# Weights of an attention layer multiplied by Strassen's scheme on pairs of row tiles, with additions moved to GpSimd and side jobs spread anew, in a two-layer graph kernel

## Chip, cores and metric

The kernel runs on one core of a Trainium2 chip. The metric is the device time of one execution in microseconds (us); the time before is the median of three runs, 2179.1 us (2177.47 to 2179.86).

## What is computed

x has 3327 rows of 512 numbers, adj is 3327 x 3327, everything in float32. With h = relu(layernorm(x)), layer 0 is graph attention and layer 1 a normalised graph convolution:

```
h = relu(layernorm(x))
q, k, v = h Wq' + bq, h Wk' + bk, h Wv' + bv
x = x + softmax(q k' / sqrt(512) + 2 adj) v
h = relu(layernorm(x))
A2 = adj + I;  ds = diagonal(A2) ** -0.5
x = x + relu((ds A2 ds) (A2 h W'))
```

## The kernel before

**Tiles.** Rows are padded to 26 tiles of 128. They are kept as two halves of 13 tiles (six pairs and one left over) and as two strips s = 0 and 1, of 14 and 12 tiles; matmuls have 448 columns for strip 0 and 384 for strip 1. `ROW` gives the order in which row tiles are finished.

**Opening (lines 273 to 379).** Wq and Wk are merged into one matrix M. For each of the 26 row tiles, `h_transposed` loads x, computes the norm (`norm`, L191: statistics on VectorE, the power -0.5 on GpSimd at L200, and on demand the bias -mean * rstd on VectorE, L204), applies relu with scale and bias on ScalarE (ACT, L323), stores h for later and transposes it on TensorE. `project_q` multiplies by M. In this part the instructions are put in order by a scheduler at build time.

**Scores (lines 384 to 577).** Products of h and q, exp, and stores of the probabilities and of sums of blocks that Strassen's scheme needs, into DRAM.

**Three big products (from line 581).** g = 0 is probabilities times h, g = 1 is A2 times h of layer 1, g = 2 is A2 times the rows of layer 1's product. Each is done by one level of Strassen's scheme over halves (seven products p5, p1, p6, p7, p2, p3, p4, `ORDER`), with a second level inside. A **step** is one of these products for one strip and one pair of row tiles: `Step`, with seven matmuls (L813) or, for the thirteenth tile, four (L805). Steps are numbered by `number_of(g, r, s, t)`: 98 for each g, 14 for each of the seven products, 7 for each strip. `Right` makes a step's right side out of stored rows, `Gather` takes the finished strip out of PSUM (`first`, `rest`) and `settle` combines strips into `cts`.

Order is written out by hand: `run(k)` issues step k's loads (for step k+3), its matmuls, and between the matmuls pieces of VectorE's work from the list `waiting` (sums of step k+2, then what `at(k, ...)` has put there); `in_order` pins each engine's instructions, including DMA issues on SP and ACT, to that order. `post` and `deliver` put ACT's stores off to the next step.

**Layer 0's weights** (what the change replaces). The result of g = 0 stands transposed in `cts`. For each row tile, at steps 79 to 108, `attend` multiplies four slices of it by Wv (`times_weights`, four matmuls of 512 columns, L905), and VectorE scales the sum by rs and adds x (L917), adds bv (L918) and takes the norm's statistics; x comes by `attend_load` on ACT's queue two steps earlier, and `attended` applies relu on ACT one step later and stores h of layer 1 (`rowd[1]`).

**Layer 1's weights.** `Temp` (L939) does the same kind of product for pairs of row tiles by seven products of half size with the blocks of W and their sums (`W`, `four_differences`), at places between matmuls given by `AFTER`: eight additions of 128x128 on VectorE (`sums`, L956), 14 matmuls of 256 columns (L966), four evictions on ACT (L970) and three on VectorE (L972).

**Side jobs.** `Job` (L881) adds a block of adj to a stored sum and stores the result, for later products of g = 1 and 2: two loads on SP, one VectorE addition (L896), one store on ACT. There are 52, evenly spread over steps 7 to 163, in four places (two jobs deep).

Of the kernel before, what the change touches and what calls it, by code (L numbers as in the profile page):

```python
# [15 lines left out]
P = 128  # L16
# [20 lines left out]
PAIRS = 6  # L37
# [10 lines left out]
def graph_layers_kernel(  # L48
# [117 lines left out]
    totd = dram.tile([1, NP], F32, name="totd")  # L166
    x1d = [dram.tile([P, D], F32, name=f"x1d{i}") for i in range(NT)]
# [23 lines left out]
    def norm(src):  # L191

        st = small.tile([P, 6], F32, name="st")
        nc.vector.bn_stats(st, src)
        mv = small.tile([P, 2], F32, name="mv")
        nc.vector.bn_aggr(mv, st)
        ve = small.tile([P, 1], F32, name="ve")
        nc.vector.tensor_scalar(ve, mv[:, 1:2], EPS, None, op0=ALU.add)  # L198
        rstd = small.tile([P, 1], F32, name="rstd")
        nc.gpsimd.tensor_tensor(rstd, ve, mhalf, op=ALU.pow)  # L200

        def bias():
            nb = small.tile([P, 1], F32, name="nb")
            nc.vector.scalar_tensor_tensor(nb, mv[:, 0:1], -1.0, rstd, op0=ALU.mult, op1=ALU.mult)  # L204
            return nb

        return rstd, bias
# [85 lines left out]
    nc.sync.dma_start(bq_sb, bq)  # L293
    M = blocks(range(4, 8), "M")
# [20 lines left out]

    def h_transposed(k):

        a, n = PACKS[k]
        for _, i in (o for o in order if o[0] == k):
# [3 lines left out]
            nc.scalar.activation(ht, xt, AF.Relu, bias=bias(), scale=rstd)  # L323
            nc.sync.dma_start(rowd[0][ROW[i]], ht)
            pt = tp_bank("tp").rearrange("p (c e) -> p c e", c=DC)
# [50 lines left out]
    for k, then in itertools.zip_longest(TURN, TURN[1:]):  # L376
        if then is not None:
            h_transposed(then)
        project_q(k)
# [240 lines left out]
    def weights(src):  # L620

        w = [half(k, [P, 2, D], "w") for k in (12, 13)]
        for c in range(DC):
            nc.sync.dma_start(w[c // 2][:, c % 2], src[c * P : (c + 1) * P])
        return [w[c // 2][:, c % 2] for c in range(DC)]

# [3 lines left out]
    bvs = []  # L630

    def prepare():
        wv_w1.append(weights(wvT))
        bvs.append(half(11, [P, D], "bv_sb"))
        nc.sync.dma_start(bvs[0], bass.AP(tensor=bv.tensor, offset=bv.offset, ap=[[0, P], [1, D]]))
        LD = adjT.shape[1]
        with nc.allow_non_contiguous_dma(reason="the diagonal, once"):
            nc.sync.dma_start(dg, bass.AP(tensor=adjT.tensor, offset=adjT.offset, ap=[[LD + 1, P], [P * (LD + 1), NT]]))

    def prepared():  # L640
        nc.vector.reciprocal(rs, tot)
        nc.vector.tensor_scalar(dg, dg, 1.0, None, op0=ALU.add)
        nc.gpsimd.tensor_tensor(sd, dg, mh, op=ALU.pow)
        nc.scalar.mul(nsd, sd, -1.0)

    wv_w1 = []
# [3 lines left out]
    def other_weights():  # L650

        b11, b21, b22, t1, t2, t3 = blocks((11, 12, 13), "w1")
        b12, t4 = (mid(k, [P, 2, E], "w1") for k in (10, 11))
        W.extend((b11, b12, b21, b22, t1, t2, t3, t4))
        for z in range(2):
            for y in range(2):
                block = w1T[z * E : (z + 1) * E, y * E : (y + 1) * E]
                nc.sync.dma_start(W[2 * z + y], block.rearrange("(c p) e -> p c e", p=P))
        differences.append(four_differences(W))
# [7 lines left out]
    nsd = const.tile([P, NT], F32, name="nsd")  # L667

# [37 lines left out]
    job_ring = ring(*spare[2:], (half, 14))  # L706
    x_slots = [lambda k=k: view(2, 1).rearrange("p a w -> p (a w)")[:, k * D : (k + 1) * D] for k in range(3)]
    x_slots = itertools.cycle([*x_slots, lambda: mid(10, [P, D], "xt")])
    h_ring = ring((mid, 11))
# [171 lines left out]
    class Job:  # L881


        def __init__(self, k, s, j):
            self.k, self.s, self.j = k, s, j

        def load(self):
            s, j, w = self.s, self.j, H[self.s]
            self.a, self.b = (job_ring([P, H[0]], "job")[:, :w] for _ in range(2))
# [11 lines left out]
    def times_weights(i, w):  # L901
        s, y, k = where(i)
        ps = bank(ROLE["p8"], "p8")
        for d in range(DC):
            nc.tensor.matmul(ps, cts[s][y][d][:, k * P : (k + 1) * P], w[d], start=d == 0, stop=d == DC - 1)  # L905
        return ps

    xts = {}

    def attend_load(i):  # L910
        xts[i] = next(x_slots)()
        nc.scalar.dma_start(xts[i], x[i * P : (i + 1) * P])

    def attend(i):

        xt, ps = xts[i], times_weights(i, wv_w1[0])
        nc.vector.scalar_tensor_tensor(xt, ps, rs[:, i : i + 1], xt, op0=ALU.mult, op1=ALU.add)  # L917
        nc.vector.tensor_add(xt, xt, bvs[0])  # L918
        post(x1d[i], xt)
        normed[i] = norm(xt)  # L920

    def attended(i):
        h1 = h_ring([P, D], "h1")
        nc.scalar.activation(h1, xts[i], AF.Relu, bias=normed[i][1](), scale=normed[i][0])
        nc.scalar.dma_start(rowd[1][i], h1)

    normed = {}

# [10 lines left out]
    class Temp:  # L939
# [10 lines left out]
        def sums(self):  # L950

            a11, a12, a21, a22 = self.blocks()
            self.o = half(14, [P, 4, 2, P], "rows")
            for k, x, y in ((1, a21, a22), (2, None, a11), (3, None, a12), (0, a11, a21)):
                for c in range(2):
                    yield nc.vector.tensor_add(self.o[:, k, c], self.o[:, {2: 1, 3: 2}[k], c] if x is None else x[c], y[c])  # L956

        def product(self, j):
            name, h, new, n, sign = PARTS[j]
            if j == 0:  # L960
                self.ps = bank(ROLE["p8"], "pw").rearrange("p (k e) -> p k e", k=2)
                self.to = [next(ts_slots)() for _ in self.its]
            left, ps = {"m1": 0, "p2": 1, "p4": 3}.get(name), self.ps[:, h]
            for c in range(2):
                a = self.o[:, {"p7": 0, "p5": 1, "p6": 2, "p3": 3}[name], c] if left is None else self.blocks()[left][c]
                nc.tensor.matmul(ps, a, W[B[name]][:, c], start=new and c == 0, stop=c == 1, skip_group_check=True)  # L966
            i = self.its[n // 2]
            to, by = self.to[n // 2][:, n % 2 * E : (n % 2 + 1) * E], (sd if sign > 0 else nsd)[:, i : i + 1]
# [4 lines left out]
            if j == len(PARTS) - 1:  # L973
                for i, ts in zip(self.its, self.to):
                    post(rowd[2][i], ts)
# [40 lines left out]
    every = (*range(PAIRS), None)  # L1016
    rights = {(g, r, t): Right(g, r, t) for g in range(3) for r in ORDER for t in every}
# [23 lines left out]
    k0, k1 = number_of(0, 0, 1, 0), number_of(1, 5, 0, 0) - 4  # L1041
    for n, job in enumerate(jobs):
        k = k0 + n * (k1 - k0) // len(jobs)
# [3 lines left out]
    def rows(g, k, i, *z):  # L1047

        if g == 0:
            at(k - 2, attend_load, i)  # L1050
            at(k, attend, i)
            at(k + 1, attended, i)
        else:
            at(k - 2, finish_load, i, *z)
            at(k, finish, i, *z)
# [3 lines left out]
    k = number_of(0, 5, 1, 2)  # L1059
    for i in ROW:  # L1060
        if steps[k].t is None:
            k += 1
        rows(0, k, i)
        k += 1
    inserted, sums_of = {}, {}
    k = number_of(1, 5, 1, 2)
    for n in range(0, NT, 2):
        if steps[k].t is None:
            k += 1
        w = Temp(*ROW[n : n + 2])  # L1070
        sums_of[k] = w.sums
        for j, (later, m) in enumerate(AFTER):
            inserted.setdefault((k + later, m), []).append((w, j))
        k += 2
# [11 lines left out]
    for t, i in enumerate(range(20, NT)):  # L1086
        rows(2, number_of(2, 4, 0, t + 2), i, (1,))
# [4 lines left out]
    k = number_of(1, 4, 0, 0)  # L1092
    at(k, other_weights)
    for n in range(4):
        at(k + 3 + n, difference)
    at(k + 8, turn_sign)
# [27 lines left out]
    def run(k):  # L1124
# [19 lines left out]
        for j, _ in enumerate(itertools.chain((None,), step.multiply(banks_of))):  # L1144
# [11 lines left out]
            elif weighs and j > 0:  # L1156
# [29 lines left out]
        while len(waiting) > added:  # L1186
            do(waiting.pop(0))

# [384 lines left out]
```

## Time and profile before

| what | value |
|---|---|
| median of three runs | 2179.1 us |
| the profiled execution's own time | 2178.22 us |
| its span (first to last instruction) | 2176.4 us |
| TensorE's granted clock | 0.997 |
| ACT busy | 238.4 us (11%) |
| L905, 512 columns, cts by Wv | part of 104 matmuls, two passes each |
| DMA moved | 583.68 MB, mean 268 GB/s |
| GpSimd pow at L200 | 52, mean 0.83 us |

Times are microseconds on one profiled execution. PE is TensorE's matmul, PEld its weight load, DVE VectorE, ACT ScalarE, POOL GpSimd, SP the engine that issues most DMAs. "Idle before" a group is what its engine stood still just before, with what ended it. Matmuls overlap, so their pace is read from the start of one to the start of the next.

### The profile page before, as it was taken

Reading aid. Unit: us, or ns where it says so; the run is one execution under the profiler, and the core shown is the slowest. Engines: PE = TensorE matmul, PEld = TensorE weight load, DVE = VectorE, ACT = ScalarE, POOL = GpSimd, SP = SyncE. Lnnn points to the kernel's source line nnn. Section 1 sums busy time; section 2 is a strip of 40 time slices with the busy share of each in tenths; the row PEclk is TensorE's granted clock in tenths of the full one; section 3 lists DMA queues with packets and bytes.
Section 4 is the critical chain, followed back from the end, with each engine's and each line's share of the span. In section 5 each row is a group of like instructions: output and inputs, shape, how many; then the busy total and the mean of one; then the engine's idle time right before and its main releaser. Section 6 shows DMA issues by size and latency. Waiting matters only on the chain.

```text
span 2176.4 us, 21093 instructions
## 1 busy us (share of the span) xinstructions
PE 2163.2 (99%) x6424; PEld 1197.1 (55%) x6424; DVE 1664.5 (76%) x3250; ACT 238.4 (11%) x363; POOL 49.0 (2%) x60
## 2 busy tenths in 40 slices
PE   9999999999999999999999999999999999999998
PEld 6555555455555555555454555555666655555555
DVE  6369888888886698886778778887676667778686
ACT  5312111121110000000000000000011100000011
POOL 2000000000000000000111000000000000000000
PEclk9999999999999999999999999999999999999999
DMA  8568888889989899888787889986646468756685
GB/s 290 177 222 308 294 298 287 294 290 310 321 290 298 291 377 331 287 296 304 259 304 263 308 277 370 320 303 219 207 145 200 142 202 276 254 188 212 218 305 194
DMA packets 300374, 583.68 MB, mean 268 GB/s; under 512 B 34518, under 2 KB 168028, under 8 KB 300252
## 3 DMA queue, kind: packets, MB, share of 16 engines
q1 hardware_dynamic: 265102, 512.76, 69.4%
q10 hardware_dynamic: 35150, 69.48, 8.7%
q8 instruction: 53, 0.87, 0.2%
q14 instruction: 69, 0.57, 0.1%
HBM read 414.28 MB, written 167.85 MB: 267 GB/s over the span
## 4 chain that ended last, share of the span: by engine, by line
PE 95%; DVE 3%; DMA 1%; issue 1%; ACT 0%; POOL 0%; DVEq 0%; POOLq 0%
PE p L813 54%; PE Y L454 13%; PE Z L454 7%; PE p L805 5%; PE p L905 4%; PE pw L966 3%; PE X L454 3%; PE Y L347 2%; PE Z L347 1%; PE mm L306 1%; DMA part<-sum 1%; PE tp L327 1%; DVE part L173 1%; PE pt L995 1%; PE X L347 0%
## 5 line engine op out<-in xcount | busy, mean ns | idle before, releaser
L813 PE MATMUL p<-part,b 128*128 128x448 f32 (+1 forms) x3528 | 1261.5, 513 | 0.3 <-DVE part L174 0.2
L813 PEld LDWEIGHTS p<-part,b 128*128 128x128 f32 x3528 | 668.1, 190 | 534.7 <-issue 284.7
L454 PE MATMUL Y<-qt,hp 128*128 128x448 f32 (+1 forms) x832 | 308.2, 513 | 0.3 <-DVE g L466 0.3
L173 DVE TENSOR_TENSOR part<-part 128x896 f32<-128x896 f32 (+1 forms) x252 | 257.0, 1020 | 65.7 <-DMA part<-p 24.0
L454 PEld LDWEIGHTS Y<-qt,hp 128*128 128x128 f32 x832 | 157.7, 190 | 134.3 <-issue 72.3
L454 PE MATMUL Z<-qt,hp 128*128 128x384 f32 (+1 forms) x416 | 162.5, 513 | 0.0
L175 DVE TENSOR_TENSOR part<-part,part 128x448 f32<-128x448 f32 (+1 forms) x219 | 129.5, 591 | 14.9
L174 DVE TENSOR_TENSOR part<-part,part 128x448 f32<-128x448 f32 (+1 forms) x219 | 129.4, 591 | 7.2
L805 PE MATMUL p<-part,b 128*128 128x448 f32 (+1 forms) x336 | 124.2, 513 | 0.0
L454 PEld LDWEIGHTS Z<-qt,hp 128*128 128x128 f32 x416 | 78.8, 190 | 67.4 <-issue 37.2
L458 DVE SCALAR_TENSOR_TENSOR g<-g,Y 128x384 f32<-128x384 f32 (+1 forms) x156 | 91.5, 587 | 31.3 <-PE Y L454 28.6
L805 PEld LDWEIGHTS p<-part,b 128*128 128x128 f32 x336 | 63.7, 190 | 53.5 <-issue 31.2
L841 ACT COPY part<-p 128x384 f32<-128x384 f32 (+1 forms) x33 | 16.6, 502 | 657.5 <-PE p L813 542.1
L454 PE MATMUL X<-qt,hp 128*128 128x384 f32 (+1 forms) x208 | 81.1, 512 | 0.0
L461 ACT ACTIVATE g<-g 128x768 f32<-128x768 f32 (+1 forms) x48 | 43.0, 896 | 347.8 <-DVE g L458 278.6
L905 PE MATMUL p<-w,ct 128*128 128x512 f32 x136 | 61.8, 594 | 0.5 <-DVE part L917 0.5
L842 DVE TENSOR_TENSOR part<-p,part 128x384 f32<-128x384 f32 (+1 forms) x33 | 19.3, 585 | 51.6 <-PE p L813 50.9
L454 PEld LDWEIGHTS X<-qt,hp 128*128 128x128 f32 x208 | 39.5, 190 | 33.1 <-issue 19.3
L200 POOL TENSOR_TENSOR rstd<-ve,mhalf 128x1 f32<-128x1 f32 x52 | 43.0, 830 | 567.9 <-DVE ve L198 538.7
L966 PE MATMUL pw<-w,rows 128*128 128x256 f32 x208 | 53.6, 380 | 0.8 <-DVE rows L956 0.8
L896 DVE TENSOR_TENSOR job<-job 128x896 f32<-128x896 f32 (+1 forms) x52 | 52.9, 1018 | 0.0
L466 DVE TENSOR_TENSOR g<-g,Z 128x384 f32<-128x384 f32 (+1 forms) x52 | 30.5, 586 | 26.8 <-PE Z L454 26.4
(176 smaller groups left out, 1697.6 us busy)
## 6 DMA issues: line engine op xcount, KB each, us to landing
part<-sum SPq DMA_DIRECT2D x104, 448.0 KB, 5.0
part<-p SPq DMA_DIRECT2D x91, 448.0 KB, 6.0
part<-sum SPq DMA_DIRECT2D x104, 384.0 KB, 3.7
part<-p SPq DMA_DIRECT2D x91, 384.0 KB, 4.4
part<-in_adjT_dram SPq DMA_DIRECT2D x78, 448.0 KB, 4.9
b<-row SPq DMA_DIRECT2D x234, 128.0 KB, 4.7
part<-in_adjT_dram SPq DMA_DIRECT2D x78, 384.0 KB, 3.5
g<-in_adjT_dram SPq DMA_DIRECT2D x52, 448.0 KB, 4.4
```

What stands on the lines that cost most here:

```text
L173: yield nc.vector.tensor_add(o[:, 0:2], g[:, 0:4:3], g[:, 1:2].to_broadcast([P, 2, g.shape[-1]]))
L174: yield nc.vector.tensor_add(o[:, 2], o[:, 1], g[:, 0])
L175: yield nc.vector.tensor_add(o[:, 3], o[:, 2], g[:, 2])
L200: nc.gpsimd.tensor_tensor(rstd, ve, mhalf, op=ALU.pow)
L347: nc.tensor.matmul(ps[:, :w], M[B[name]][:, c, o * P : (o + 1) * P], hp[k][:, A[name], c], start=start and c == 0, stop=c == 1, skip_group ...
L454: nc.tensor.matmul(ps[:, :wd], h_of(self.t, name, k), qt[B[name]][:, k], start=start and k == 0, stop=k == 1, skip_group_check=True)
L458: nc.vector.scalar_tensor_tensor(a[n], a[n], 2.0, ps[:, :wd], op0=ALU.mult, op1=ALU.add if sign > 0 else ALU.subtract)
L805: yield nc.tensor.matmul(ps[("p2", "p3", "p4", "p8")[k]][:, :w], b[:, z], a[:, 0, y], start=k == 3, stop=True)
L813: yield nc.tensor.matmul(ps[r][:, :w], b[:, i], m, start=self.t == 0, stop=self.t == PAIRS - 1 and r in ("p1", "p5", "p6", "p7"))
L896: nc.vector.tensor_add(self.a, self.a, self.b)
L905: nc.tensor.matmul(ps, cts[s][y][d][:, k * P : (k + 1) * P], w[d], start=d == 0, stop=d == DC - 1)
L966: nc.tensor.matmul(ps, a, W[B[name]][:, c], start=new and c == 0, stop=c == 1, skip_group_check=True)
```

## The change

Seven things are changed together.

1. Layer 0's product with Wv is done by the class that does layer 1's: `Temp` becomes `Weighed` with two kinds, `Attend` and `Temp`; `Attend` works on pairs of row tiles with Wv in blocks, at the same places between matmuls.
2. Wv's blocks, their sums and the turned sign are loaded and made at steps 56 to 64 (`load_weights`), not at step 2; nrs = -rs is added beside nsd.
3. bv is loaded in the opening; GpSimd adds it to x there (`add_bv`, two tiles behind the norms) and SP stores the sum in `xbd`. `Attend` loads that sum in place of x, and GpSimd adds it to the finished product.
4. `norm` makes the bias at once, on GpSimd; VectorE gets a small operation for -mean.
5. The norm of a pair comes at its second step or one later, relu and the store of h three steps after the pair's first step (`ends`).
6. The 52 side jobs are split: 23 over steps 7 to 73, 29 over steps 112 to 171, each run with six places (three jobs deep).
7. VectorE's pieces are held back for one more matmul at a strip's first step.

```diff
@@ norm
+        nm = small.tile([P, 1], F32, name="nm")
+        nc.vector.tensor_scalar(nm, mv[:, 0:1], -1.0, None, op0=ALU.mult)
         rstd = small.tile([P, 1], F32, name="rstd")
         nc.gpsimd.tensor_tensor(rstd, ve, mhalf, op=ALU.pow)
-        def bias():
-            nb = small.tile([P, 1], F32, name="nb")
-            nc.vector.scalar_tensor_tensor(nb, mv[:, 0:1], -1.0, rstd, op0=ALU.mult, op1=ALU.mult)
-            return nb
-        return rstd, bias
+        nb = small.tile([P, 1], F32, name="nb")
+        nc.gpsimd.tensor_tensor(nb, nm, rstd, op=ALU.mult)
+        return rstd, nb
@@ opening
+    bv_sb = mid(4, [P, D], "bv_sb")
+    nc.sync.dma_start(bv_sb, bass.AP(tensor=bv.tensor, offset=bv.offset, ap=[[0, P], [1, D]]))
+    def add_bv():
+        i, xt = normed.pop(0)
+        nc.gpsimd.tensor_tensor(xt, xt, bv_sb, op=ALU.add)
+        nc.sync.dma_start(xbd[ROW[i]], xt)
@@ h_transposed
+            normed.append((i, xt))
+            if len(normed) > 2:
+                add_bv()
@@ products with Wv
-    def attend(i):
-        xt, ps = xts[i], times_weights(i, wv_w1[0])
-        nc.vector.scalar_tensor_tensor(xt, ps, rs[:, i : i + 1], xt, op0=ALU.mult, op1=ALU.add)
-        nc.vector.tensor_add(xt, xt, bvs[0])
-        post(x1d[i], xt)
-        normed[i] = norm(xt)
+    class Attend(Weighed):
+        factors, slots = (rs, nrs), x1_slots
+        def places(self):
+            return [piece(10 + k, D, D + 2 * P).rearrange("p (c e) -> p c e", c=2) for k in range(4)]
+        def load(self):
+            self.x = [next(x_slots)() for _ in self.its]
+            for i, x in zip(self.its, self.x):
+                nc.scalar.dma_start(x, xbd[i])
+        def done(self):
+            for i, x1, x in zip(self.its, self.to, self.x):
+                nc.gpsimd.tensor_tensor(x1, x1, x, op=ALU.add)
+                post(x1d[i], x1)
+        def norm(self):
+            self.norms = [norm(x1) for x1 in self.to]
+        def finish(self):
+            for i, x1, x, (rstd, bias) in zip(self.its, self.to, self.x, self.norms):
+                nc.scalar.activation(x, x1, AF.Relu, bias=bias, scale=rstd)
+                nc.scalar.dma_start(rowd[1][i], x)
@@ places of pairs and jobs
-    k0, k1 = number_of(0, 0, 1, 0), number_of(1, 5, 0, 0) - 4
+    first_job, first_row = number_of(0, 0, 1, 0), number_of(0, 5, 1, 2)
+    later_job, last_job = number_of(1, 1, 0, 0), number_of(1, 5, 0, 0) + 4
     for n, job in enumerate(jobs):
-        k = k0 + n * (k1 - k0) // len(jobs)
+        if n < EARLY:
+            k = first_job + n * (first_row - 5 - first_job) // EARLY
+        else:
+            job.late = True
+            k = later_job + (n - EARLY) * (last_job - later_job) // (len(jobs) - EARLY)
+            if g == 0:
+                at(k + 1, w.load)
+                at(k + 1 + (steps[k + 1].t == PAIRS - 1), w.norm)
+                ends[k + 3] = w.finish
+    for k, src in ((number_of(0, 4, 0, 0), wvT), (number_of(1, 4, 0, 0), w1T)):
+        at(k, load_weights, src)
@@ run
-            elif weighs and j > 0:
+            elif weighs and j > (1 if t == 0 else 0):
                 do(first_of(waiting), 2)
+        if k in ends:
+            ends[k]()
```

## The prediction

> **What bounds the kernel now.** I read first the page's busy times, then the chain that ended last, then the groups of instructions, then stretches of the span.
>
> ```profile
> PE 2163.2 (99%) x6424; PEld 1197.1 (55%) x6424; DVE 1664.5 (76%) x3250; ACT 238.4 (11%) x363; POOL 49.0 (2%) x60
> PE 95%; DVE 3%; DMA 1%; issue 1%; ACT 0%; POOL 0%; DVEq 0%; POOLq 0%
> ```
>
> TensorE (PE) is busy for 99% of the 2176.4 us and makes 95% of the chain. Busy is not a proof of full pace, so I compared starts of successive matmuls: 0.376 us for a pass of 448 columns, 0.323 for 384, almost everywhere (each float32 matmul is two passes in the trace). So only two things can move the time: passes taken off TensorE, and new holes in its stream. The stretch of the products with Wv, in the chain in order of time:
>
> ```profile
> 1047.75 0.18 issue
> 1047.93 0.75 DVE part L917
> 1048.68 0.04 issue
> 1048.73 3.70 PE p L905 x8
> 1052.43 5.26 PE p L813 x14
> 1057.69 3.43 PE p L905 x8
> ```
>
> A row tile's product with Wv is 8 passes of 512 columns in 3.43 us, 0.429 each. It stands between two steps of 14 passes (5.26 us). One hole is visible: at 1048 the product waited for VectorE (DVE), which came from a side job (L896) just before; it is 0.63 us over the pass's own time. Holes of the stretch from 1000 to 1240 us sum to 1.3 us. The scheme that the change brings in runs already, in layer 1 (L966, TensorE's part of the timeline):
>
> ```profile
> 1580.97 1.03 PE L966 MATMUL pw<-w,rows 128*128 128x256 f32 x4
> 1581.84 1.67 PE L813 MATMUL p<-part,b 128*128 128x448 f32 x4
> ```
>
> Four passes of 256 columns take 1581.84 - 1580.97 = 0.87 us, 0.217 each (0.216 is the middle value of the trace). Last, the stretches:
>
> ```profile
> 1000.00:1240.00 240.00, 239.38 (x642) 121.53 (x641) 182.50 (x369) 23.64 (x31) 26.92 (x26) 1.00 0.84 285
> 1530.00:1765.00 235.00, 233.97 (x812) 153.13 (x811) 151.11 (x357) 26.67 (x57) 0.00 (x0) 1.00 0.54 176
> 1315.00:1330.00 15.00, 15.00 (x42) 7.56 (x41) 13.00 (x27) 0.00 (x0) 0.00 (x0) 1.00 1.02 386
> ```
>
> Columns: length, busy PE, weight loads, DVE, ACT, POOL, granted clock, DMA share, GB/s. DVE is at 76% with Wv and 64% in layer 1's weight stage; layer 1's p6 has the DMA engines full at 386 GB/s.
>
> **What the Trainium skill says.** GPSIMD Engine Reference, section 3.1, gives 4497 ns for a tensor_tensor add of 2048 float32 and about 2.6 cycles an element; for 512 my estimate from it is 512 x 2.6 / 1.2 GHz = 1.11 us and 0.06 of dispatch, 1.17. The trace has no such add; VectorE's own takes 0.69 (L918). SBUF, section "Who interferes with whom": a VectorE instruction with two SBUF inputs and a GpSimd instruction that reads SBUF exclude each other for the whole instruction. The trace agrees as far as it goes:
>
> ```profile
> 1050.46 1.09 DVE L173 TENSOR_TENSOR part<-part 128x896 f32<-128x896 f32 x1
> 1050.68 1.28 POOL L200 TENSOR_TENSOR rstd<-ve,mhalf 128x1 f32<-128x1 f32 x1 [14.79 <-DVE ve L198]
> ```
>
> The pow takes 0.55 us with VectorE idle, 1.28 beside L173: it waits for the rest of L173 (0.87 us) and needs 0.41 more. No row shows VectorE held up by GpSimd. TensorE: Matmul & The Clock Gate, section "Architectural detail: the array is 16× 32×32, not 1× 128×128", says that VectorE's queue is strictly first in, first out; so whatever waits in it holds what stands behind.
>
> **The change, part by part.**
>
> Products with Wv. Removed: 26 tiles x 8 passes x 0.429 = 89.2 us. Added: 13 pairs x 7 products x 2 halves x 2 passes = 364 passes x 0.216 = 78.6 us. All of it is in TensorE's stream: **-10.6 us**. This holds whatever else happens.
>
> VectorE in that stage, a pair of tiles at strips of 448, from starts in the timelines. Before: two steps' sums 2 x 2.33, two tiles with L917, L918, norm and nb 2 x 2.63, two right sides of p4 (L780 and four differences) 2 x 1.65, 0.67 job at 1.1: 14.0 us in 2 x 5.26 + 16 x 0.429 = 17.4 us of TensorE, 80%. After: 4.66, eight sums of 128x128 at 0.20 = 1.62, three L972 at 0.39 = 1.17, two norms with one more small op 2.22, right sides 3.30, no job: 13.0 in 10.53 + 28 x 0.216 = 16.6 us, 78%. If each of the pair's two GpSimd adds locks VectorE out for its full 1.17 us, 15.3, 92%. So it is no new bound on average. But the coupling is tighter. A product adds into the PSUM half that ACT or VectorE must have read about 3 us earlier (p5 after p2, p6 after m1), and p5 needs sums that VectorE makes in the same step. Layer 1 shows the price: its 13 pairs have 2.6 us of holes, nearly all where VectorE also gathers and settles a finished strip. Here VectorE has the norms too, but no diagonals (L795). I take 4 us of holes, against 1.3 now: **+2.7** (from -1, if the job-made hole goes and none comes, to +18, the slower rival).
>
> x + bv, ahead of time. VectorE loses 26 L918; GpSimd gets 26 adds in the opening and 26 in the stage. ACT's load of x + bv is issued at the start of a pair's second step; such loads land after 5.4 us (part<-in_x_dram). That step's last product ends after 5 matmuls of 0.75 and 3 products of 0.87, at 6.4 us of 7.9; ACT reads it by 6.9, and GpSimd's second add ends about 1 us into the next step. The norm's bn_stats waits for it. In VectorE's queue it stands behind the next pair's first L972, which waits for TensorE until 3.2 us into that step, and behind that pair's eight sums: some 4 us after the add, so I cost the wait at nothing. If that cover is gone, pair sums and L972 wait behind bn_stats, and TensorE behind those.
>
> The opening. GpSimd has 26 pows (0.55) now; it gets 26 bias products (between 0.41, what the pow above needs, and 0.55, the pow alone; I take 0.5) and 26 adds of 1.17: 17 us become 60 in the 50 us in which norms run. The adds may trail by two tiles and beyond. SP's queue gets 26 stores of 256 KB, and an x slot (11 of them) comes free only after its store, some 5 us later than now. Covers: x loads run several tiles ahead, and the last 8 tiles' norms stand ready by 49 us, well before their transposes. In return VectorE no longer waits in its queue for the pow (8.3 us in 10 waits for L204); TensorE's holes from 24 to 31 us (some 4 us) hang on that chain of norm, ACT and copies. **0**, between -2 and +4. bv's slot also holds back one early adjacency load, from 12 us to about 70; it is used at 112: nothing.
>
> Bias on GpSimd in the stage: one more product of 0.5 behind each pow; ACT uses it a step later. Nothing. ACT: 4 evictions of 0.47 more a pair, about 21% busy. Nothing.
>
> Wv as blocks: the same 1 MB, at step 56 in place of 2; four differences of 0.7 us on VectorE in g = 0, where slices are at 10 to 15.5 of 16 us; nrs and the sign on ACT. SP's queue loses five DMAs at step 2. Nothing; cover gone, under 1.
>
> Side jobs. Before: 52 in 157 steps, 0.33 a step, from step 7 to 164. After: 23 in 67 steps (0.34), none in the Wv stage, then 29 in 60 steps (0.48) from step 112. Six places make three jobs deep in place of two, so the slots are reused after 8.7 and 6.2 steps, against 6: SP's waits for a job's store (30.0 us over 9 waits, up to 7.4) shrink. The cost is in layer 1's p1 and p6: 0.15 job a step x 1.3 MB in 4.6 us = 42 GB/s more, where 1300 to 1390 us runs at 337 to 388 GB/s with share 0.96 to 1.02. Now, p6 has one hole of 0.43 us at 1331. By jobs counted step by step, the backlog there grows by about 0.5 MB around steps 121 to 127, 1.3 us at 385 GB/s, and drains more slowly; left operands are loaded three steps ahead (14 us), right ones five. **+0.5**, between -0.4 (the hole goes) and +8 (3.1 MB undrained).
>
> Sum: -10.6 + 2.7 + 0 + 0.5 = -7.4. On the profiled execution, 2178.2 us with its span of 2176.4 and 1.8 around it, 2170.8; the median of the three runs is 0.9 above that execution: **2171.7 us**.
>
> **Rivals.**
>
> All of it arrives: VectorE has room, since the jobs have left the stage, the stage keeps its 1.3 us of holes, and the opening gains 1 from the freed VectorE queue: -11.6, 2167.5. For: 78% in place of 80%. Against: layer 1's 2.6 at 64%.
>
> The gain is eaten elsewhere: p6 of layer 1 loses 4 us to full DMA engines and the opening 2 to late x and GpSimd's queue: -10.6 + 2.7 + 6 = -1.9, 2177.2. For: share 1.02 over 30 us. Against: g = 0's p6 runs at up to 403 GB/s with no hole.
>
> Slower: bn_stats waits in VectorE's queue for GpSimd's add. One mechanism: x lands late or the add waits for the port behind 1.09 us sums, VectorE stands, pair sums and L972 slip, TensorE's next p5 or p6 waits. At one add and its wait (1.17 + 0.2) a pair it is 13 x 1.37 = 17.8: -10.6 + 17.8 = +7.2, 2186. It turns the sign by more than the bound from (10.6 + 4.4) / 13 = 1.15 us a pair. Against: the 4 us of cover above.
>
> **How the numbers follow.** 0.2% is 4.4 us, about what a measurement of this kernel tells from no change. Forecast 0.50 (gain 4.4 to 9), all arrives 0.20, eaten 0.18, slower 0.12. Faster 0.70, same 0.18, slower 0.12. The range 2166.5 to 2180.5 takes in the first three and cuts the slower one.
>
> **What would show it.** Right: passes of 256 columns at 0.216 in the stage, where before stood 0.429; holes there of 2 to 6 us in all, at strips' ends; no bn_stats wait on POOL above 1 us; GpSimd's 512-wide add at 1.1 to 2.2 us. Wrong: VectorE waiting for POOL in the stage, with TensorE behind it; holes between 1290 and 1400 above 2 us, released by DMA; more than 5 us of holes before 120 us.

## The result and the profile after

The median of four runs is **2196.6 us** (2195.48 to 2197.37), against 2179.5 for the kernel before on the same chip: a ratio of 1.0080, 95% interval 1.0068 to 1.0093. The forecast was 2171.7; the change makes the kernel slower by 17 us. The profiled execution took 2195.5 us, its span is 2193.5 us, and the granted clock 0.996.

The page's busy times and the shares of its chain, after:

```profile
PE 2160.1 (98%) x6580; PEld 1228.5 (56%) x6580; DVE 1684.7 (77%) x3345; ACT 263.0 (12%) x417; POOL 118.4 (5%) x164
PE 89%; DMA 4%; DVE 4%; POOL 1%; issue 1%; ACT 1%; SPq 0%; ACTq 0%; POOLq 0%; DVEq 0%
```

PE had 95% of the chain and has 89% now; the shares of DMA, DVE and POOL have grown, so something other than TensorE ends last in more places than before. To find where, I took every matmul pass of both traces, subtracted from its start-to-start distance the pass's own pace (0.376 us for 448 columns, 0.323 for 384, 0.429 for 512, 0.216 for 256), and summed what is left, by phase. These are TensorE's **holes**, in us; g0, g1 and g2 are the big products, with the two weight stages cut out of them. A pass that ran at a lowered clock adds its lost time to them (see the last section):

| kernel | opening | scores | g0 | Wv stage | g1 | W stage | g2 | all |
|---|---|---|---|---|---|---|---|---|
| before | 7.3 | 1.7 | 1.8 | 1.3 | 0.4 | 2.6 | 0.1 | 15.2 |
| after | 15.8 | 1.7 | 2.8 | 10.9 | 9.4 | 2.8 | 0.1 | 43.5 |

Holes grew by 28.2 us, passes fell by 10.6, what follows the last matmul fell by 0.5: together 17.1, and the spans differ by 2193.5 - 2176.4 = 17.1. So the gain on passes came, and three phases ate it: the opening (+8.5), the Wv stage (+9.6), g1 (+9.0), with +1.0 in g0.

**Opening.** The chain that ended last, at 50 to 60 us of the kernel after (start, length, what):

```profile
53.76 0.82 ACT ht L331
...
54.65 0.78 POOL xt L321
...
55.88 0.55 POOL rstd L203
...
56.51 0.20 POOL nb L205
...
56.73 0.82 ACT ht L331
```

One tile goes round in 3 us: relu on ACT, GpSimd's add of bv (which overwrites x, so it waits for that relu), then the next tile's power and bias, then its relu. The source calls an add two tiles after its norm, but in the order that the scheduler made at build time that lag is gone here: the seventeenth add (54.65) comes right behind the seventeenth tile's power (52.92) and relu (53.76), and ahead of the eighteenth power (55.88), which stands behind it in GpSimd's queue. The waits show it from the other side (engine, line, what it waited for: us in total, times, longest), first after, then before:

```profile
POOL xt L321 <- ACT ht L331: 10.0, 12, 1.2
DVE st L195 <- DMA xt<-in_x_dram: 20.9, 12, 6.4
```

```profile
DVE st L194 <- DMA xt<-in_x_dram: 9.4, 4, 6.4
```

x comes later too, since its place comes free only when the add is done and the sum is stored. The last norm's power is at 83.5 us; before, at 57.9.

**Wv stage.** VectorE's timeline after, around the first large hole (the norms are L195 to L201, L960 is a product's read-out):

```profile
1050.01 1.82 DVE L890 TENSOR_TENSOR part<-part,part 128x768 f32<-128x768 f32 x2
1051.75 0.68 DVE L796 TENSOR_TENSOR b<-b,rows 128x512 f32<-128x512 f32 x1
...
1053.40 0.69 DVE L195 BATCH_NORM_STATS2 st<-piece 128x6 f32<-128x512 f32 x1
...
1054.47 0.68 DVE L195 BATCH_NORM_STATS2 st<-piece 128x6 f32<-128x512 f32 x1
...
1055.54 0.48 DVE L960 SCALAR_TENSOR_TENSOR piece<-pw,rs,piece 128x256 f32<-128x256 f32 x1
```

and TensorE's:

```profile
1051.48 1.03 PE L954 MATMUL pw<-wv,piece 128*128 128x256 f32 x4
1052.34 1.67 PE L829 MATMUL p<-part,b 128*128 128x448 f32 x4
1056.07 1.13 PE L954 MATMUL pw<-wv,piece 128*128 128x256 f32 x4 [2.06 <-DVE piece L960]
```

The product p3 ends at 1052.3; four passes later, at 1053.84, p7 should start, but it waits for p3's read-out. That one stands in VectorE's queue behind the end-of-strip settling (L890), a right side (L796 and four differences) and the two norms of the pair before, 2.1 us. In the program p7 and p3 add into different halves of the PSUM bank. Still, in all 26 pairs of the two weight stages no product starts before the read-out of the one just before it has ended (0.05 us after it at the closest). Nothing in VectorE's queue waits; it is simply full. The windows (columns as in the prediction) say the same: on the whole stage VectorE is as busy as before, in these 18 us it is at 97%:

```profile
1000.00:1240.00 240.00, 232.34 (x802) 151.35 (x801) 184.38 (x442) 44.86 (x80) 58.13 (x78) 1.00 0.67 220
1044.00:1062.00 18.00, 15.26 (x51) 9.30 (x50) 17.51 (x43) 3.05 (x5) 2.08 (x4) 1.00 0.77 264
```

**g1.** After, the chain of 1360 to 1390 us runs over loads of operands, then over VectorE:

```profile
1371.59 7.05 DMA rows<-row
...
1378.65 4.31 DMA b<-row
1382.96 0.70 DVE b L796
...
1384.62 1.09 DVE part L912
1385.71 0.48 DVE part L874
...
1386.23 3.84 PE p L829 x5
```

In the chain a right side's rows take 7.05 us (loads of rows have medians of 4.6 and 4.8 over the whole run) and a load of b 4.31 (median 4.9); then VectorE makes the right side, a side job (L912) and then the strip's take-out (L874) that frees PSUM for TensorE. The stretch after, and the same stretch of the kernel before:

```profile
1240.00:1400.00 160.00, 153.81 (x431) 82.16 (x430) 128.33 (x236) 4.03 (x7) 0.18 (x1) 0.99 0.97 349
```

```profile
1240.00:1400.00 160.00, 159.84 (x452) 85.49 (x452) 130.00 (x239) 2.55 (x5) 0.00 (x0) 1.00 0.92 331
```

The DMA share rose from 0.92 to 0.97 as a mean over 160 us, with windows of 1.02 and 1.03 in it: little is left to catch up with.

### The profile page after: what moved, and what is told of

It is laid out like the page before. It is cut to its first block, busy times and chain, and to the rows that moved or that the text cites. A ratio compares the mean times of both kernels' runs of the same rounds, so it can differ in the third digit from the quotient of the medians.

```text
span 2193.5 us, 21848 instructions
## 1 busy us (share of the span) xinstructions
PE 2160.1 (98%) x6580; PEld 1228.5 (56%) x6580; DVE 1684.7 (77%) x3345; ACT 263.0 (12%) x417; POOL 118.4 (5%) x164
## 4 chain that ended last, share of the span: by engine, by line
PE 89%; DMA 4%; DVE 4%; POOL 1%; issue 1%; ACT 1%; SPq 0%; ACTq 0%; POOLq 0%; DVEq 0%
PE p L829 52%; PE Y L468 13%; PE Z L468 7%; PE pw L954 6%; PE p L821 5%; PE X L468 3%; PE Y L358 1%; DMA rows<-row 1%; DMA part<-sum 1%; PE mm L307 1%; DVE part L174 1%; DMA b<-row 1%; PE pt L1022 1%; POOL xt L321 0%; PE Z L358 0%
## 5 line engine op out<-in xcount | busy, mean ns | idle before, releaser
L176 DVE TENSOR_TENSOR part<-part,part 128x448 f32<-128x448 f32 (+1 forms) x219 | 132.5, 605 | 14.6
L175 DVE TENSOR_TENSOR part<-part,part 128x448 f32<-128x448 f32 (+1 forms) x219 | 133.4, 609 | 7.3
L954 PE MATMUL pw<-wv,piece 128*128 128x256 f32 x208 | 54.3, 382 | 6.1 <-DVE piece L960 5.0
L954 PEld LDWEIGHTS pw<-wv,piece 128*128 128x128 f32 x208 | 39.1, 190 | 27.2 <-DVE piece L960 7.1
L358 PE MATMUL Y<-hp,M 128*128 128x384 f32 (+1 forms) x128 | 50.5, 526 | 0.0
```

What stands on the lines that cost most here:

```text
L175: yield nc.vector.tensor_add(o[:, 2], o[:, 1], g[:, 0])
L176: yield nc.vector.tensor_add(o[:, 3], o[:, 2], g[:, 2])
L358: nc.tensor.matmul(ps[:, :w], M[B[name]][:, c, o * P : (o + 1) * P], hp[k][:, A[name], c], start=start and c == 0, stop=c == 1, skip_group ...
```

## The experiments

**Theory:** three separate causes, one for each phase: GpSimd's adds and their stores in the opening, the norms in VectorE's queue in the stage, the crowding of side jobs in g1. **Rivals:** GpSimd's add holding up the norms in the stage (the prediction's slower case), and one common cause, such as full DMA engines. All results, as medians; the holes of phases that an edit doesn't touch also vary from build to build of the kernel after (opening 13.0 to 16.0, g0 1.7 to 5.4, stage 10.7 to 13.8, g1 9.4 to 11.3), so only larger differences are read:

| run | us | ratio to before (95%) | opening | g0 | stage | g1 |
|---|---|---|---|---|---|---|
| e1_no_add_early | 2187.7 | 1.0037 (1.0024 to 1.0050) | 6.4 | 2.7 | 11.7 | 9.8 |
| e6_add_on_dve | 2193.2 | 1.0064 (1.0047 to 1.0081) | 12.0 | 3.8 | 11.4 | 9.7 |
| e9_add_no_store | 2192.0 | 1.0051 (1.0034 to 1.0068) | 10.8 | 3.4 | 12.2 | 10.2 |
| f3_before_add_bv | 2189.7 | 1.0050 (1.0033 to 1.0067) | 17.4 | 2.2 | 1.2 | 0.0 |
| e7_no_norm | 2189.6 | 1.0048 (1.0031 to 1.0065) | 14.8 | 1.7 | 3.9 | 10.4 |
| e2_norm_later | 2200.7 | 1.0097 (1.0080 to 1.0114) | 13.6 | 1.7 | 15.5 | 11.3 |
| e8_stage_add_on_dve | 2210.2 | 1.0139 (1.0122 to 1.0156) | 13.7 | 5.4 | 24.3 | 11.3 |
| e3_jobs_32_20 | 2194.8 | 1.0068 (1.0051 to 1.0085) | 14.2 | 11.2 | 10.7 | 2.3 |
| e10_jobs_27_25 | 2191.0 | 1.0049 (1.0032 to 1.0066) | 13.0 | 7.6 | 12.4 | 2.4 |
| f2_before_jobs_23_29 | 2186.8 | 1.0034 (1.0020 to 1.0048) | 7.8 | 2.7 | 0.0 | 10.0 |
| h1_job_loads_on_act | 2192.2 | 1.0063 (1.0046 to 1.0080) | 15.7 | 2.1 | 11.0 | 5.9 |
| h2_job_loads_on_pool | 2192.9 | 1.0061 (1.0044 to 1.0078) | 16.0 | 2.4 | 12.6 | 4.7 |
| h3_job_loads_third_less | 2186.1 | 1.0031 (1.0020 to 1.0043) | 14.2 | 2.2 | 13.8 | 0.0 |
| f1_three_causes_off | 2175.4 | 0.9984 (0.9975 to 0.9992) | 6.7 | 5.6 | 3.3 | 1.7 |
| g1_repaired | 2188.9 | 1.0043 (1.0030 to 1.0057) | 11.3 | 6.2 | 12.4 | 3.0 |

### The opening

**e1.** The kernel after without the opening's add and its store:

```diff
-            normed.append((i, xt))
-            if len(normed) > 2:
-                add_bv()
...
-                nc.scalar.dma_start(x, xbd[i])
+                nc.scalar.dma_start(xt, x[i * P : (i + 1) * P])
```

> The changed kernel without x + bv in the opening: no GpSimd additions of 128x512 there, no stores of the sums, and the Wv stage loads x itself. It leaves bv out of the result. Theory: the additions and their stores make the opening's holes on TensorE (16.0 us before 100 us in the changed kernel, 7.5 in the kernel before); they fall to 7 to 8, the time by 8.5, from 2196.6 to 2188. Rival: the bias product on GpSimd and the extra small VectorE operation, which stay here, make them; then the opening keeps 14 us or more and the time stays above 2194.

Measured: 8.9 us less than after, holes of 6.4 in the opening, below the kernel before's 7.3. The bias product on GpSimd, which is still there, shows no cost.

**e6** makes the same add on VectorE, **e9** keeps it on GpSimd and leaves out the store:

```diff
-        nc.gpsimd.tensor_tensor(xt, xt, bv_sb, op=ALU.add)
+        nc.vector.tensor_tensor(xt, xt, bv_sb, op=ALU.add)
```

```diff
         nc.gpsimd.tensor_tensor(xt, xt, bv_sb, op=ALU.add)
-        nc.sync.dma_start(xbd[ROW[i]], xt)
```

> The changed kernel with the opening's x + bv on VectorE in place of GpSimd; stores and places as they are. Theory of GpSimd's queue (each pow and bias product stands behind an addition of 1.27 us): the opening's holes fall from 16.0 to 8 to 10, time 2189 to 2191. Rival theory of the x slots (a slot comes free only after the store of the sum, so x comes late): holes stay at 14 or more, time above 2194.

> The changed kernel with the opening's GpSimd additions but without the 26 stores of the sums; the Wv stage loads x (bv is left out of the result). Moving the additions to VectorE took 3.9 us of the opening's 15.8 us of holes away, leaving both out 9.4. Theory that both matter, GpSimd's queue about 4 and late x slots behind stores about 5: holes fall to 10 to 12, time 2191 to 2193. Rival: GpSimd's queue alone holds the norms up and the stores ride along: holes stay above 14.

Measured: holes 12.0 with the adds on VectorE, 10.8 without the stores, 6.4 without both (e1), 15.8 with both. e6 missed both its expectations (2193.2 us lies between them), e9 came as its theory of two causes said. The wait for x falls from 20.9 us to 8.5 in e6, though the stores are still there, and to 11.3 in e9. So add and store work together, and taking away either removes some 4 to 5 us. The sizes are rough: 12.0 lies only 1.0 below what builds show that don't touch the opening, and e6 also loads VectorE's queue.

**f3** is the other direction, the kernel before with this add and store alone:

```diff
+            raw.append((i, xt))
+            if len(raw) > 2:
+                add_bv()
```

> The kernel before with the opening's part of the add alone: bv is loaded, GpSimd adds it to each x two tiles behind the norms, and SP stores the sum, which nothing reads; the norm's bias stays on VectorE, everything else as before. If adds and stores make the opening's cost by themselves, the opening's holes rise from 7.3 us to 14 to 16 and the time to 2187 to 2188. If it takes GpSimd's bias product as well (so that each relu waits in GpSimd's queue behind an add), the holes rise to 10 or 11 and the time to 2182 to 2184.

Measured: 17.4 us of holes, 1.6 of them passes at a lowered clock, and +10.8 us, both above the first expectation. The add and the store, with the load of bv, make the whole cost, without the bias product on GpSimd.

### The Wv stage

**e7** leaves the norms out of the stage:

```diff
-            self.norms = [norm(x1) for x1 in self.to]
+            pass
...
-                nc.scalar.activation(x, x1, AF.Relu, bias=bias, scale=rstd)
+                nc.scalar.activation(x, x1, AF.Relu, bias=pad, scale=1.0)
```

> The changed kernel without the 26 norms of the Wv stage: relu is applied with a fixed bias and scale, so layer 1's h is not normalised (that part is left out). Theory: VectorE's work at a strip's end is too much for the 3 us that a product leaves for its read-out, and the norms (2.1 us a pair) are what tips it; the stage's holes fall from 10.9 us to 3 to 4 (the weight stage of layer 1 has 2.8), the time from 2196.6 to 2189.5. Rival: the bunch of gather, settle and right sides alone does it, or GpSimd's additions do: holes stay above 7.

Measured: the stage falls from 10.9 to 3.9 us of holes, the time by 7.0. The products, the sums and GpSimd's adds are all still there.

**e8** moves the stage's add of x from GpSimd to VectorE, ahead of the norm. If VectorE's waiting for GpSimd were the trouble, this would help; if the length of VectorE's queue is, it harms.

```diff
         def done(self):
+            pass
+
+        def norm(self):
             for i, x1, x in zip(self.its, self.to, self.x):
-                nc.gpsimd.tensor_tensor(x1, x1, x, op=ALU.add)
+                nc.vector.tensor_tensor(x1, x1, x, op=ALU.add)
                 post(x1d[i], x1)
...
```

> The changed kernel with the Wv stage's additions of x on VectorE, just ahead of each norm, in place of GpSimd. Theory of VectorE's queue: 1.45 us more in front of the read-out at each of the strips' ends, holes of the stage rise from 10.9 to 14 to 16, time 2200. Rival, GpSimd's hold on the port: the holes at 1119 and 1224 us (1.3 us, where a 128x128 addition took 1.36 us beside GpSimd's) and more go, the stage falls below 9.5.

Measured: 24.3 us of holes, the direction of the queue theory and more than it expected. The two additions of a pair, ahead of its norms, made holes so long that TensorE's granted clock fell to 0.50 after them (1057 to 1063 us and 1173 to 1176 us; see the last section). The passes at that clock are 4.7 of the 24.3 us.

**e2** puts the norm and the relu of the pair that ends a strip one step later:

```diff
-                at(k + 1 + (steps[k + 1].t == PAIRS - 1), w.norm)
-                ends[k + 3] = w.finish
+                late = steps[k + 1].t == PAIRS - 1
+                at(k + 1 + 2 * late, w.norm)
+                ends[k + 3 + late] = w.finish
```

> The changed kernel with the norm and the relu of the pair that ends a strip (second step t = 5) one step later. Theory: the holes of the Wv stage (11.0 us against 1.3) come from VectorE's queue: after a strip's end two norms (2.1 us) stand with settle and a right side ahead of the p3 read-out that TensorE waits for; one step later they do not. Holes of the stage fall by 6 to 7, the time from 2196.6 to 2190. Rival: GpSimd's additions hold the port that VectorE needs; then the holes move by less than 2 us.

Missed: 15.5 us of holes, the time 2200.7. The hole of 2.2 us ahead of p7 is gone, but p4, the next product, now waits 1.8 us (0.8 after) for p7's read-out, and a hole of 2.95 us comes behind it, released by another engine. The chain there:

```profile
1057.73 1.46 POOL rstd L203
...
1060.73 0.82 ACT piece L1001
...
1062.03 0.48 ACT piece L958
...
1062.55 1.13 PE pw L954 x4
```

The norm now comes so late that its relu (L1001) waits in ACT's queue, and the next pair's eviction (L958) behind it; TensorE waits for that. The power itself (L203) took 1.46 us in place of 0.55. Moved, the stall changed its name.

### The side jobs

**f2** is the kernel before with the changed kernel's places of the jobs alone (23 and 29, six places):

```diff
-        k = k0 + n * (k1 - k0) // len(jobs)
+        if n < EARLY:
+            k = first_job + n * (first_row - 5 - first_job) // EARLY
+        else:
+            k = later_job + (n - EARLY) * (last_job - later_job) // (len(jobs) - EARLY)
...
```

> The kernel before with the changed kernel's side jobs alone: 23 over steps 7 to 73, 29 over steps 112 to 171, six places, none in the Wv stage; products with Wv, norms and opening as before. If the crowding of the jobs alone makes the holes of g1, they appear here: 8 to 11 us in g1, 1 to 3 in g0, at most 1.3 in the Wv stage, and about 2188. If they come from what the new product with Wv does to g1 (later rows of layer 1, VectorE), g1 keeps less than 2 us of holes and the time stays at 2178 to 2181.

Measured: 10.0 us of holes in g1, none in the stage (its job-made hole is gone), +8.0 us. The same stretch as above:

```profile
1240.00:1400.00 160.00, 153.24 (x427) 81.13 (x426) 126.97 (x234) 2.02 (x4) 0.00 (x0) 0.99 0.95 344
```

PE 153.24 of 160 us, as in the kernel after (153.81), though the product with Wv is the old one. The new places of the jobs alone make it.

**e3** and **e10** share the jobs out otherwise: `EARLY` is 32 and 27 in place of 23.

> The changed kernel with 32 side jobs in the first run and 20 in the second, in place of 23 and 29 (0.48 and 0.33 a step in place of 0.34 and 0.48). Theory: full DMA engines in layer 1's p1 and p6 make the holes between 1300 and 1390 us (9.5 against 0.4); with the old rate there they fall to 0.5 to 1.5, and layer 0, where the page shows spare share, gains at most 2: 2196.6 to 2188 to 2190. Rival: layer 0's p6 is as full (0.98 to 1.04), the holes move there and the time stays within 2 us.

> The changed kernel with 27 side jobs in the first run and 25 in the second (0.40 and 0.42 a step). With 23 and 29 the holes of g = 0 and of g = 1 ahead of layer 1's weights are 2.8 and 9.4 us, with 32 and 20 they are 11.2 and 2.3, in the kernel before (0.33 and 0.33) 1.8 and 0.4. Theory that full DMA engines in p6 set a limit that bends upward: in the middle both are small, 3 to 5 and 3 to 5, the sum 7 to 9 in place of 12.2, time 2192 to 2194. Rival: bytes are delayed in proportion and the sum stays at 12 to 13.

Measured: with 32 the holes move to g0 (11.2 and 2.3), the rival's case; with 27 they are 7.6 and 2.4. The sum is 12.2, 10.0 and 13.5 for 23, 27 and 32, so 27 lies between its two expectations; the kernel before, which also uses the stage's 38 steps, has 2.2. Each place that is relieved hands its holes to the other. Six places in place of four were not tried by themselves; with six places at the rate of before (e3's later run, 0.33 a step) g1 has 2.3 us against 0.4, so they explain 2 us there at most.

What lacks, throughput or order? **h1** and **h2** issue the jobs' two loads on ACT and on GpSimd, which keeps the bytes and takes them out of SP's order (h1's edit first; h2 has `nc.gpsimd` there); **h3** leaves out the load of adj's block:

```diff
-            nc.sync.dma_start(self.a, sumd[s][j][:, 1 + self.k])
-            nc.sync.dma_start(self.b, adjT[r0 : r0 + P, c0 : c0 + w])
+            nc.scalar.dma_start(self.a, sumd[s][j][:, 1 + self.k])
+            nc.scalar.dma_start(self.b, adjT[r0 : r0 + P, c0 : c0 + w])
```

```diff
-            nc.sync.dma_start(self.b, adjT[r0 : r0 + P, c0 : c0 + w])
...
-            nc.vector.tensor_add(self.a, self.a, self.b)
+            nc.vector.tensor_add(self.a, self.a, self.a)
```

> The kernel after with the side jobs' two loads issued by ACT in place of SP; same bytes, same places, same steps. If SP's in-order issue is what makes the holes, the operands' loads no longer stand behind a job: g1 falls from 9.4 us of holes to 2 to 4, time 2190 to 2192. If the DMA engines' throughput is what lacks, g1 keeps 7 to 11 us and the time stays at 2195 to 2198. ACT may itself stand at such an issue and read out a product late; that would show as TensorE waiting for ACT.

> The kernel after with the side jobs' two loads issued by GpSimd, whose queue has nothing else in g1. SP's order as cause: g1 at 2 to 4 us of holes, 2190 to 2192. Throughput as cause: g1 at 7 to 11 us, 2195 to 2198.

> The kernel after without the load of adj's block in the side jobs: VectorE adds the stored sum to itself, so that these sums are other numbers; a job moves 0.9 MB in place of 1.3. All else as in the kernel after; job traffic per step of the later run becomes what the kernel before had (0.48 x 0.9 against 0.33 x 1.3 MB). Throughput as cause: g1's holes fall to 0 to 1.5, g0's to 1 to 2, time 2186 to 2188. SP's order as cause: one of a job's two issues is gone, the wait for its place stays, so g1 keeps 4 to 7 us, time 2191 to 2194.

Measured: h3's g1 has no hole; with 0.4 MB a job less, the stretch is

```profile
1240.00:1400.00 160.00, 160.00 (x458) 86.51 (x457) 137.84 (x257) 4.02 (x7) 0.76 (x2) 1.00 0.94 337
```

h3 takes away a third of the jobs' bytes, and with them half of their load issues; VectorE's additions stay. h1 and h2 keep the bytes and take all these issues off SP, and 5.9 and 4.7 us of the 9.4 stay. So about half is a matter of bytes that no change of order removed, and a third fewer bytes remove it all. The other part, some 4 us, seems to be that operands' loads stand behind the jobs' in SP's queue; h1 and h2 fall between their two expectations. The Trainium skill (DMA: Bandwidth & Descriptors, section "Issuing engines are not separate DMA queues") says that starting DMAs on several engines saves only the sequencer's time for starting them. That much agrees: the bytes still bind. Here the order of issue seems to be worth nearly half as well; why was not tried by itself.

### All three together

**f1** takes all three causes away: e1, e7 and `EARLY = 27` in one kernel (without bv, and without layer 1's norm).

> The kernel after with the three suspected costs taken away together: no add of bv in the opening (x is loaded by Attend, so bv is left out of the result), no norms in the Wv stage (layer 1's h is not normalised), and 27 of the 52 side jobs in the early run in place of 23. If the three costs are independent, their single gains add up: 2196.6 - 8.9 - 7.0 - 5.6 = 2175, with holes of 6 to 7.5 us in the opening, 3 to 5 in the Wv stage and 9 to 11 in g0 and g1 together. If they are one thing seen three times (full DMA engines, say), the reliefs overlap and the time stays at 2182 or more, with a phase whose holes are above these.

Measured: 2175.4, the sum of the single gains to within the interval, so they are not one thing seen three times. By phases the agreement is looser: of e10's 5.6 us, 2.8 are holes of the opening, which it does not touch, and its g0 and g1 together fell by 2.2; in f1 they fell by 4.9. Even with these reliefs, and without two parts of the computation, the kernel is only 0.16% faster than the kernel before (ratio 0.9984, 0.9975 to 0.9992), since 7.3 us of holes stay in g0 and g1, against 2.2 before.

**g1** is a whole kernel with repairs in all three phases: the add on VectorE, `EARLY = 27`, and the end-of-strip norms put behind the fourth matmul of the next pair's first step:

```diff
-                at(k + 1 + (steps[k + 1].t == PAIRS - 1), w.norm)
+                if steps[k + 1].t == PAIRS - 1:
+                    within[k + 3] = [(w.norm, ())]
+                else:
+                    at(k + 1, w.norm)
```

> The kernel after, whole, with three repairs in three phases: the opening's add on VectorE, 27 side jobs in the early run, and the norms of the pair that ends a strip put into the next pair's first step after its fourth matmul, behind the read-outs that TensorE waits for first, with relu at that step's end as now. Queue theory: the three gains add up, 3.5 for the opening, 5.6 for the jobs, and the stage's holes fall from 10.9 to 4 to 6 us because no norm stands ahead of a read-out and relu still has 4 us after its norm: about 2182, so at best level with the kernel before. Rival: VectorE has no room there at all, the norms now delay that step's sums and right sides, and the stage keeps 9 to 12 us of holes: about 2187 to 2188.

Measured: the opening (11.3) and the jobs (6.2 and 3.0) came nearly as expected, the stage did not: 12.4, the rival's case. VectorE at the same place as above:

```profile
1048.35 0.68 DVE L195 BATCH_NORM_STATS2 st<-piece 128x6 f32<-128x512 f32 x1
...
1050.76 1.82 DVE L890 TENSOR_TENSOR part<-part,part 128x768 f32<-128x768 f32 x2
1052.50 0.68 DVE L796 TENSOR_TENSOR b<-b,rows 128x512 f32<-128x512 f32 x1
...
1055.66 1.57 DVE L175 TENSOR_TENSOR part<-part,part 128x448 f32<-128x448 f32 x1
...
1058.41 0.47 DVE L960 SCALAR_TENSOR_TENSOR piece<-pw,rs,piece 128x256 f32<-128x256 f32 x1
```

The two norms (1047.29 to 1049.42) no longer stand directly ahead of the read-out at 1054.15, but ahead of the settling and the right side, which still lie between; a sum (L175) takes 1.57 us in place of 0.62 beside GpSimd's add (1055.26 to 1056.75), and TensorE has holes of 1.9 and 1.8 us, where after had 2.2 and 0.8. At the same place e7, without the norms, has 0.1 and 0.8. So the norms don't fit at this place either; that no other order would fit is not shown.

## Why the prediction was wrong

Its first step, the passes, was right. Three terms of the sum failed: the stage's distance, the opening's covers and the jobs' backlog.

- **Products, -10.6: right.** The passes have 256 columns at 0.216 us, 364 of them; the balance of the spans closes with that figure.
- **Holes of the stage, +2.7; measured +9.6.** The average was right: VectorE 184.38 of 240 us, 77%, forecast 78. The failed term is the distance. "A product adds into the PSUM half that ACT or VectorE must have read about 3 us earlier": the trace shows p7 waiting for the read-out of p3, the product just before it, and p7 is due 1.5 us after p3's end. And 4 us were taken from layer 1's 2.6 with "Here VectorE has the norms too, but no diagonals", as if these balanced. They do not: e7 prices the norms at 7.0 us, and what stays without them (3.9) is near layer 1's 2.8. The queue was nearly as full there before the change (17.37 of 18 us at 1038 to 1056), but a product of a whole tile had a step between two read-outs.
- **The slower rival: right in sign, wrong in mechanism.** bn_stats never waited for GpSimd. Its row in the groups by shape, idle time last:

```profile
L195 DVE BATCH_NORM_STATS2 st<-piece 128x6 f32<-128x512 f32 x26 | 17.8, 684 | 0.1
```

The cover of 4 us held. What harmed is the norms' own 2.1 us for a pair in VectorE's queue, and e8 shows that taking GpSimd out of it makes it worse.
- **The opening, 0 (-2 to +4); measured +8.5.** The working had 60 us of GpSimd in 50 us and dismissed it with "The adds may trail by two tiles and beyond". In the order that was built they don't: an add that waits for its relu holds the next tile's power and bias. The stores' effect was seen ("some 5 us later") and covered by "the last 8 tiles' norms stand ready by 49 us". That was misread in the kernel before too: there six of the 26 powers come between 51.5 and 57.9 us, and after the last comes at 83.5. The gain set against it was misread as well: of the 3.9 us of holes from 24 to 31 us only 1.1 hang on a wait. The rest is the clock, which is 0.51 there (a pass of 384 columns takes 0.640 us), and the holes are the same after (4.0). By e6 and e9 add and store share the cost, each with some 4 to 5 us.
- **Side jobs, +0.5 (-0.4 to +8); measured +9.0 in g1, +1.0 in g0.** The first hole at 1314 us is 1.3 us, as the working's backlog; but it was taken as paid once. With the share at 0.98 to 1.04 from 1300 to 1390 us the backlog came back at 1335 (1.0) and 1379 to 1390 (2.0, 2.3, and 1.9 at a low clock). The bound of +8 was the better value; f2 and h3 show it. That the stage's own job-made hole goes, which the working had only at the end of a range, came true in f2 (0.0).
- **Bias on GpSimd, weights as blocks, ACT's evictions: nothing each.** Nothing speaks against it, but no run tries them singly. e1's opening is no worse than before's; f2, without the blocks, has 2.7 us in g0, the kernel after 2.8; the stage without norms has 3.3 to 3.9 us (f1, e7), 2.0 to 2.6 above before, for the closer read-outs and these parts together.
- **The rival "eaten elsewhere"** named two of the three phases with the right mechanisms, full DMA engines and late x with GpSimd's queue, but at 4 and 2 us in place of 9.0 and 8.5; the prediction gave it 0.18. Of the prediction's signs of being wrong, holes between 1290 and 1400 us came. More than 5 us of holes before 120 us came too, but was no sign: the kernel before has 7.3 us in its opening.
- GpSimd's add takes 1.27 us alone (estimated 1.17), the bias product 0.19 (taken as 0.5): sizes that decided nothing.

What stays open: why p7 waits for p3's read-out although their halves differ; how g1's 9.4 us divide exactly between throughput and SP's order, since h1, h2 and h3 don't add up (4 and 9.4); and what the change's seventh part does, which no run tries by itself.

## What to carry to other kernels

An engine's average load says little about a hand-ordered stage: find the read-out that the bound engine waits for, count what stands ahead of it in its queue at the worst place (here a strip's end), and compare with the distance to the next use. Work that is called a side job and fills gaps has a price only where there are none: taking its places away in one stage (here 38 steps at a DMA share of 0.84) puts its bytes where the share is already 1. And work moved to an idle engine is free only if nothing short and urgent, like a norm's power, comes behind it in that engine's queue; look at the order that was built, not at the lag that the source intends.

## What the runs showed of the hardware

**A hole can cost more than its length.** After the holes of 2.0 and 2.3 us at 1379 and 1384 of the kernel after, TensorE's passes of 448 columns took 0.746 us in place of 0.376; the granted clock there:

```profile
1386.00:1389.50 3.50, 3.27 (x5) 1.62 (x6) 3.43 (x7) 0.00 (x0) 0.00 (x0) 0.54 1.06 391
```

From 35 us after the start to 15 us before the end the seventeen traces have 22 such falls of the clock to 0.50, 20 of 3.41 us and two of 6.83 (e7 and e8); a fall of 3.41 us costs up to 1.7. All come inside a hole of at least 2.0 us or within 1.4 us of its end. Not every such hole brings one: the kernel after has a hole of 2.2 us up to 1056 and e2 one of 2.95 us up to 1062.5, both with the clock at 1.00 behind them, while h3, after 2.04 us at the first of these places, fell to 0.50 from 1054.15 to 1057.57. What decides is not shown. The Trainium skill (TensorE: Matmul & The Clock Gate, section "What's actually happening") has the clock halved after an idle window of about 3.4 us. The half pace and the length of 3.41 us agree; the trigger does not, since 19 of the 22 falls came after holes of 2.0 to 2.6 us.

This explains a good part of the stage's differences between the nine builds that don't touch it: without what their passes lost at the low clock (0 to 3.3 us), the holes of 10.7 to 13.8 us become 9.0 to 11.1, in eight of them 9.8 to 11.1.

**The shared port locks VectorE too.** The prediction had seen only GpSimd held up. In the stage after:

```profile
1118.74 1.55 DVE L944 TENSOR_TENSOR piece<-ct,ct 128x128 f32<-128x128 f32 x2
1118.88 1.27 POOL L992 TENSOR_TENSOR piece<-piece,part 128x512 f32<-128x512 f32 x1 [7.66 <-issue]
```

Two 128x128 additions, 0.48 us together where GpSimd is idle (at 1046.48 us), take 1.55 beside GpSimd's add. That agrees with the Trainium skill (SBUF — State Buffer, section "Who interferes with whom"), where a VectorE instruction with two SBUF inputs and a GpSimd instruction that reads SBUF exclude each other. TensorE had a hole of 0.55 us just behind it; during the large hole at 1054 no VectorE instruction was stretched.
